# Merging the second chunk of an attention sum over one block of nodes, two rows at a time

## The chip, the cores and the metric

The kernel runs on one core of one Trainium2 chip. The metric is the device time of one execution in microseconds, lower is better. Five engines work in parallel, each through its own queue of instructions in program order: TensorE (PE, matmuls), VectorE (DVE), ScalarE (ACT), GpSimd (POOL) and SyncE (SP, transfers). PE writes only to PSUM, a small accumulation memory; everything else lives in SBUF.

## The reference

The input is x, 64 graphs of 256 nodes with 128 features, and one 256 x 256 adjacency matrix. Four layers follow, each after a layer norm and a relu, each added onto x. The change concerns layer 0 alone, a graph attention whose score of a pair of nodes needs all 256 hidden features:

```python
    s1 = jnp.einsum('bkf,ef->bke', x, W1)
    s2 = jnp.einsum('bkf,ef->bke', x, W2)
    pre = s1[:, :, None, :] + s2[:, None, :, :] + b_lin
    h = jnp.where(pre >= 0, pre, ALPHA * pre)
    e = jnp.einsum('bije,e->bij', h, a) + bias
    attn = jax.nn.softmax(e, axis=2)
    out = jax.nn.sigmoid(jnp.einsum('bij,bjf->bif', attn, x))
```

For every graph that is a tensor of 256 x 256 x 256 (receiver i, sender j, feature e) that goes through a leaky relu and is summed over e with the weights a. Layer 1 is a gated aggregation with elu, layer 2 a tanh-capped attention, layer 3 five steps of a gated recurrence; they take the rest of the time.

## The kernel before

**Layer 0's algebra.** The leaky relu is split into a linear part, which is one matmul with v2_rep, and 0.8 times a relu, up to terms that the softmax ignores. The absolute value of a[e] is folded into the weights, so that only the sign of a[e] is left for the sum over features. The features are permuted (place, perm): those with a positive a come first, and neighbours in this order fall into the same partition of two chunks, chunk 0 holding the even places and chunk 1 the odd ones. Sign by sign the two chunks then agree in every partition, except in one if the number of positive signs is odd: the odd column. In the kernel before, this column is zeroed in chunk 1 (a_abs1) and its share is brought back for both blocks of nodes by the row term left and the matrix left2: in senders, two instructions at L570 per graph add min(left_ps, bound) to the adjacency and give adj_l, which softmax0 adds to the scores at L755.

**A tile.** For a receiver node i and a chunk, a tile of 128 features x 256 senders holds max(s2, -s1[i]). The 256 receivers are two blocks (ic = 0, 1) of 128 nodes, and a block is four groups (g) of 32 nodes. A row t takes the nodes 32 g + t of both blocks: eight tiles per chunk, held in one buffer r of 128 x 4 x 2 x 256 (there are 11). ACT makes a tile with a relu (L687), POOL with tensor_scalar (L692), and DVE makes all eight, or four, in one instruction (L669).

**A batch.** One filled buffer is a batch. PE sums it over the features with four matmuls of 512 columns (L740), one for each group g. The stationary operand is a window of 32 columns of a_win, which holds plus or minus 0.8 in its column t and zeros elsewhere, so that the result falls into row t of the group's 32 rows of e_ps. A graph's scores accumulate in e_ps over all its batches.

**Merging.** A row needs one batch for each chunk, or a single batch if chunk 1 is added onto chunk 0's tile before PE reads it. Pairs.begin merges a row if at least SPARE = 5 finished batches wait for PE. DVE then adds chunk 1's tile onto chunk 0's tile in one instruction (Pairs.merge, L709), eight times for a row; that instruction makes chunk 1's tile as it adds it.

**The order of the work.** The order is written by a planner when the program is built (manual_schedule). It keeps a clock for each engine (class Model, with costs such as TILE, WHOLE, HALF, MERGE and BATCH in ns), and always emits the step that can start first: a step of one of the chains (generators that hold the small steps of the layers: ahead for the next graph's head and senders, behind for softmax0, others for layers 1 to 3), a batch for PE, a merge for DVE, or a new tile for a free ACT, POOL or DVE. All graphs' layer-0 work is thus spread over the whole execution, and the other layers' steps lie between its batches on each engine. The helper mm (L109) issues every other matmul as four of 32 output columns.

Of the kernel before, what the change touches and what calls it, by code (L numbers as in the profile page):

```python
# [27 lines left out]
def flat(t):  # L28
    return t.rearrange("p a b -> p (a b)")
# [26 lines left out]
def kernel(ctx: ExitStack, tc: tile.TileContext, ins: dict, out: bass.AP):  # L56
# [32 lines left out]
    def dve(n, pointers=0, more=0):  # L89
        model.op("dve", 66 + n * 1.042 + 60 * pointers + more)  # L90
        return nc.vector
# [128 lines left out]
    def constants0():  # L220
# [7 lines left out]
        def col(name):  # L228
            return constant([P, 2], name)
# [21 lines left out]
        dve(2).tensor_tensor(dif, bef[:, 0:2], neg_pl, ALU.subtract)  # L251
        dve(2).tensor_tensor(dif, dif, sgn, ALU.mult)
        dve(2).tensor_tensor(place, dif, neg_pl, ALU.add)

        last, a_abs1 = col("last"), col("a_abs1")
        dve(2).tensor_scalar(last, place, n_pos, None, ALU.is_equal)
        dve(2).tensor_tensor(a_abs1, a_abs, last, ALU.mult)
        dve(2).tensor_tensor(a_abs1, a_abs, a_abs1, ALU.subtract)
        perm = lent([P, 2, 2, P], "perm", "e_t", 2)
        for src in range(2):  # L260
            for c, size in ((0, a_abs), (1, a_abs1)):
                dve(P).tensor_scalar(
                    perm[:, src, c, :], places[:, c, :], place[:, src : src + 1],
                    size[:, src : src + 1], ALU.is_equal, ALU.mult,
                )
        yield "pe"
        b_ps = psum([P, 2], "blin_ps")
# [40 lines left out]
            dve(1).tensor_scalar(w, w, 1.6, -0.8, ALU.mult, ALU.add)  # L308


        odd = constant([P, 1], "odd")
        dve(1).tensor_scalar(odd, p_two[:, 1:2], n_pos, None, ALU.is_equal)
        yield "pe"
# [4 lines left out]
        dve(1).tensor_copy(odd_all, p)  # L318
        left, left_n, left_nb = col("left"), col("left_n"), col("left_nb")
        dve(2).tensor_tensor(left, a_col, last, ALU.mult)  # L320
        dve(2).tensor_scalar(left, left, odd_all, 0.8, ALU.mult, ALU.mult)
        dve(2).tensor_scalar(left_n, left, -1.0, None, ALU.mult)
        dve(2).tensor_tensor(left_nb, left_n, blin, ALU.mult)
        for c in range(2):
# [233 lines left out]
    def senders(b, of, to):  # L558

        h_t = flat(of["h_t"][:, 2 * b : 2 * b + 2, :])  # L560
        if "bound" not in of:
            yield from bounds(of)
        yield "pe", settled
        p = psum_h([P, N], "left_ps")
        mm(p, lhsT=left2, rhs=h_t, start=True, stop=True)
        for ic in range(2):
            yield "dve", None, of["bound_at"]
            if ic == 0:
                adj_l = ap.tile([P, 2, N], F32, tag="adj_l", name="adj_l", bufs=3)
            dve(N, 1).scalar_tensor_tensor(  # L570
                adj_l[:, ic, :], p, of["bound"][:, 2 * b + ic : 2 * b + ic + 1], adj_n[:, ic, :],
                ALU.min, ALU.add,
            )
        to["adj_l"] = adj_l
        if "s2" in to:
            return
        yield "pe"
        p = psum_h([P, 2, N], "s2_ps")
        for ec in range(2):
            mm(p[:, ec, :], lhsT=w_p[:, 1, bass.ts(ec, P)], rhs=h_t, start=True, stop=True)  # L580
        yield "act"
        s2 = ap.tile([P, 2, N], F32, tag="s2", name="s2")
        act(2 * N).copy(s2, p)
        to.update(s2=s2, s2_ps=p)

    class Pairs:

        def __init__(self, g, b, of, snd):
            self.g, self.b, self.of, self.snd = g, b, of, snd
            self.row = 0
            self.todo = []
            self.merges = []
            self.batches = []
            self.opened = False
            self.owned, self.by_act = {}, 0

            self.s1n_v = of["s1n"][:, :, bass.ts(b, N)].rearrange(  # L600
                "p c (k g t) -> p c g k t", k=2, g=4
            )

        def more(self):
            return self.todo or self.row < 32
# [4 lines left out]

        def begin(self):
            waiting = sum(x["halves"] == 2 for x in self.batches)
            merged = waiting >= SPARE
            for ec in range(1 if merged else 2):
                batch = {"t": self.row, "ec": ec, "merged": merged, "halves": 0, "ready": 0.0}
                self.todo += [(batch, ec, 0), (batch, ec, 1)]
            self.row += 1

        def finished(self):

# [21 lines left out]
            batch["halves"] += 1  # L642
            batch["ready"] = max(batch["ready"], model.t[who] + LAG[who])

        def nodes(self, t, g2):

            return [
                (g, ic, self.b * N + ic * P + 32 * g + t)
                for g in (2 * g2, 2 * g2 + 1) for ic in range(2)
            ]  # L650

        def make(self, who):

            if not self.todo:
                self.begin()
            batch, ec, g2 = self.todo.pop(0)
            if g2 == 0:
                batch["r"] = rp.tile([P, 4, 2, N], F32, tag="r", name="r")
                self.batches.append(batch)
            r, t = batch["r"], batch["t"]  # L660
            s2 = self.snd["s2"] if who == "pool" else self.own(who)
            s1, s1n = self.of["s1"], self.of["s1n"]
            if who == "dve":
                whole = g2 == 0 and self.todo and self.todo[0][0] is batch
                if whole:
                    self.todo.pop(0)
                n = 4 if whole else 2
                model.op("dve", model.WHOLE if whole else model.HALF)
                nc.vector.tensor_tensor(  # L669
                    r[:, 2 * g2 : 2 * g2 + n, :, :],  # L670
                    s2[:, ec : ec + 1, :].unsqueeze(1).to_broadcast([P, n, 2, N]),
                    self.s1n_v[:, ec, 2 * g2 : 2 * g2 + n, :, t : t + 1].to_broadcast([P, n, 2, N]),
                    ALU.max,
                )
                if whole:
                    if batch["merged"]:
                        self.merges.append((model.t[who] + LAG[who], batch, 0))
                        g2 = 1
                    else:
                        self.whole(batch, who)  # L680
            else:
                for g, ic, i in self.nodes(t, g2):
                    if g > 2 * g2 or ic:
                        yield
                    if who == "act":
                        model.op("act", model.TILE["act"] + 42 * (s2 is self.snd["s2"]))
                        nc.scalar.activation(  # L687
                            r[:, g, ic, :], s2[:, ec, :], AF.Relu, bias=s1[:, ec, i : i + 1]
                        )
                    else:  # L690
                        model.op("pool", model.TILE["pool"])
                        nc.gpsimd.tensor_scalar(  # L692
                            r[:, g, ic, :], s2[:, ec, :], FLT_MAX, s1n[:, ec, i : i + 1],
                            ALU.min, ALU.max,
                        )
            if batch["merged"]:
                self.merges.append((model.t[who] + LAG[who], batch, g2))
            else:
                self.whole(batch, who)

        def merge(self):

            _, batch, g2 = self.merges.pop(0)
            r, t = batch["r"], batch["t"]
            for g, ic, i in self.nodes(t, g2):
                if g > 2 * g2 or ic:
                    yield
                model.op("dve", model.MERGE)
                nc.vector.scalar_tensor_tensor(  # L709
                    r[:, g, ic, :], self.own("dve")[:, 1, :], self.of["s1n"][:, 1, i : i + 1],  # L710
                    r[:, g, ic, :], ALU.max, ALU.add,
                )
            self.whole(batch, "dve")
# [16 lines left out]
        def multiply(self):  # L730
            if not self.opened:
                self.open()
                self.opened = True
            batch = self.next_batch()
            self.batches.remove(batch)
            self.over = not self.batches and not self.more()
            t, r = batch["t"], batch["r"]
            model.op("pe", model.BATCH)
            for g in range(4):
                nc.tensor.matmul(  # L740
                    self.e_ps[bass.ts(g, 32), :, :].rearrange("p a b -> p (a b)"),
                    lhsT=a_win[:, batch["ec"], 31 - t : 63 - t], rhs=flat(r[:, g, :, :]),
                    start=False, stop=self.over, skip_group_check=True,
                )

    def softmax0(g, b, of, e_ps, snd):

# [2 lines left out]
        for ic in range(2):  # L750
            yield "dve", lambda: "adj_l" in snd

            if ic == 0:
                nmax = sp.tile([P, 2], F32, tag="nmax", name="nmax")
            dve(N, more=10).tensor_tensor_reduce(  # L755
                e_ps[:, ic, :], e_ps[:, ic, :], snd["adj_l"][:, ic, :], -1.0, FLT_MAX,
                ALU.add, ALU.min, nmax[:, ic : ic + 1],
            )
        for ic in range(2):
# [529 lines left out]
```

## Time and profile before

| | |
|---|---|
| median of three runs | 5038.96 us (5033.29, 5038.96, 5039.4) |
| the profiled execution | 5032.98 us |
| its span, first to last instruction | 5031.1 us |
| mean granted TensorE clock | 0.999 |
| instructions DVE / ACT / POOL | 9026 / 12984 / 10725 |
| matmul records (two for each program matmul) | 57307 |
| bytes moved | 28.02 MB, mean 6 GB/s |

A line of the page's groups gives line, engine and operation, written tile <- read tiles, shapes and count, then busy time in us and the mean ns of one, then the idle time of the engine just before such instructions and what ended most of it. Busy time counts a moment once even where instructions of one engine overlap. The timeline merges equal instructions that follow each other on an engine: start in us, the time from the first start to the last end, engine, line, names, shapes and count. A row of waits gives who waited for whom, us in total, how often, and the longest.

### The profile page before, as it was taken

To read this page: it belongs to the slowest core of one execution; us is meant where nothing else is said; L and a number is where in the kernel's file an instruction comes from. 1 tells how busy PE (TensorE), PEld (TensorE's weight loads), DVE (VectorE), ACT (ScalarE), POOL (GpSimd) and SP (SyncE) were. 2 spreads that over 40 slices of the span, in tenths; PEclk is the share of its full clock that TensorE was granted. 3 is DMA by queue.
4 is the path that set the end of the run, shared out by engine and by line. 5 is a ranking of instruction groups with operands and counts; after the bars stand their busy time and mean duration, and the time that the engine had idled before them with its cause. 6 is when DMAs were issued, how large, how long until landed. Compare 5 with 4: busy or idle time off the path is not lost. (4 is left out here: it accounts for less than half of the span.)

```text
span 5031.1 us, 151796 instructions
## 1 busy us (share of the span) xinstructions
PE 4975.7 (99%) x57307; PEld 1949.9 (39%) x57307; DVE 4926.9 (98%) x9026; ACT 4945.2 (98%) x12984; POOL 4817.0 (96%) x10725
## 2 busy tenths in 40 slices
PE   9999999999999999999999999999999999999998
PEld 3334433333334333343333333333333443333433
DVE  9999999999999999999999999999999999999995
ACT  8999999999999999999999999999999999999995
POOL 8999999999999999999999999999999999999991
PEclk9999999999999999999999999999999999999999
DMA  0000000000000000000000000000000000000000
GB/s 23 4 5 2 5 6 6 6 2 6 6 6 6 2 6 6 6 6 2 6 6 6 6 2 6 6 6 6 4 6 6 6 4 3 5 4 4 4 4 8
DMA packets 56017, 28.02 MB, mean 6 GB/s; under 512 B 20336, under 2 KB 55280, under 8 KB 55280
## 3 DMA queue, kind: packets, MB, share of 16 engines
q1 hardware_dynamic: 54736, 18.04, 1.5%
q8 instruction: 449, 7.36, 0.6%
q14 instruction: 288, 2.36, 0.2%
q10 hardware_dynamic: 544, 0.26, 0.0%
HBM read 9.84 MB, written 8.45 MB: 4 GB/s over the span
## 5 line engine op out<-in xcount | busy, mean ns | idle before, releaser
L692 POOL TENSOR_SCALAR r<-s,s1n 128x256 f32<-128x256 f32 x10100 | 4567.7, 476 | 55.7 <-PE e_ps L740 28.0
L687 ACT ACTIVATE r<-s_act,s 128x256 f32<-128x256 f32 x9736 | 4360.0, 1073 | 4.6 <-PE e_ps L740 4.3
L740 PE MATMUL e_ps<-r,a_win 128*32 128x512 f32 x27824 | 3251.8, 593 | 8.8 <-DVE r L709 4.0
L669 DVE TENSOR_TENSOR r<-s_ps,s1n 128x2048 f32<-128x2048 f32 (+1 forms) x1210 | 2120.7, 1790 | 0.8 <-POOL r L692 0.8
L709 DVE SCALAR_TENSOR_TENSOR r<-s_ps,s1n,r 128x256 f32<-128x256 f32 x4944 | 2013.3, 471 | 0.2
L740 PEld LDWEIGHTS e_ps<-r,a_win 128*32 128x32 f32 x27824 | 918.8, 110 | 1721.4 <-issue 1290.3
L687 ACT ACTIVATE r<-s,s 128x256 f32<-128x256 f32 x512 | 318.8, 1234 | 0.0
L458 ACT ACTIVATE h<-x,bsh,brs 128x128 f32<-128x128 f32 x384 | 264.3, 1040 | 10.5 <-POOL bsh L452 5.0
L109 PE MATMUL m_ps<-adj_t,hn 128*32 128x256 f32 x4096 | 253.6, 381 | 1.1 <-ACT hn L1066 1.1
L1025 ACT ACTIVATE m_ps<-gate_ps,br 128x512 f32<-128x512 f32 (+1 forms) x170 | 194.7, 1145 | 14.2 <-PE gate_ps L109 13.1
L1045 ACT ACTIVATE hv_ps<-hv_ps,bh 128x512 f32<-128x512 f32 (+1 forms) x170 | 198.7, 1169 | 7.2 <-PE hv_ps L109 7.2
L1043 ACT ACTIVATE gate_ps<-gate_ps,bz 128x512 f32<-128x512 f32 (+1 forms) x170 | 203.8, 1200 | 1.1 <-PE gate_ps L109 1.1
L1015 ACT COPY m_t<-m_ps 128x512 f32<-128x512 f32 (+1 forms) x170 | 193.9, 1140 | 6.1 <-PE m_ps L109 5.6
L109 PEld LDWEIGHTS m_ps<-adj_t,hn 128*32 128x32 f32 x4096 | 140.0, 110 | 126.2 <-issue 46.1
L109 PE MATMUL gate_ps<-m_t,t_w_w 128*32 128x512 f32 (+1 forms) x1360 | 172.7, 572 | 2.6 <-ACT m_t L1015 2.2
L109 PE MATMUL gate_ps<-m_t,w_t 128*32 128x512 f32 (+1 forms) x1360 | 172.5, 568 | 2.5 <-ACT m_ps L1025 2.4
L109 PE MATMUL hv_ps<-rh,u_th 128*32 128x512 f32 (+1 forms) x1360 | 172.1, 567 | 2.1 <-DVE rh L1028 2.0
L109 PE MATMUL hv_ps<-m_t,t_w_w 128*32 128x512 f32 (+1 forms) x1360 | 172.4, 568 | 0.0
L1066 ACT COPY hn<-hn_ps 128x512 f32<-128x512 f32 (+1 forms) x136 | 153.2, 1127 | 8.7 <-PE hn_ps L116 8.6
L109 PE MATMUL gate_ps<-hf,u_t 128*32 128x512 f32 (+1 forms) x1088 | 141.9, 571 | 0.0
L109 PE MATMUL s_ps<-h0t,w_p 128*32 128x256 f32 (+1 forms) x1568 | 136.2, 446 | 1.2 <-ACT h0t L474 0.5
L450 POOL TENSOR_TENSOR brs<-bve,neg_half 128x4 f32<-128x4 f32 (+1 forms) x136 | 133.5, 982 | 0.0
(214 smaller groups left out, 4781.2 us busy)
## 6 DMA issues: line engine op xcount, KB each, us to landing
xt<-in_x_dram SPq DMA_DIRECT2D x30, 256.0 KB
out_dram<-y SPq DMA_DIRECT2D x30, 256.0 KB
row<-rows SPq DMA_DIRECT2D x128, 0.5 KB
xt<-in_x_dram SPq DMA_DIRECT2D x4, 128.0 KB
out_dram<-y SPq DMA_DIRECT2D x4, 128.0 KB
bound<-row SPq DMA_DIRECT2D x30, 2.0 KB
raw_L_gnn_w_w<-in_L_gnn_w_w_dram SPq DMA_DIRECT2D x3, 128.0 KB
adj_n<-in_adj_dram ACTq DMA_DIRECT2D x1, 256.0 KB
```

What stands on the lines that cost most here:

```text
L109: nc.tensor.matmul(out[bass.ts(c, 32), :], lhsT=lhsT[:, bass.ts(c, 32)], rhs=rhs, **flags)
L458: act(P, 2, 1).activation(h[:, g, :], xt[:, g, :], AF.Relu, bias=shift[:, g : g + 1], scale=rstd[:, g : g + 1],)
L669: nc.vector.tensor_tensor(r[:, 2 * g2 : 2 * g2 + n, :, :], s2[:, ec : ec + 1, :].unsqueeze(1).to_broadcast([P, n, 2, N]), self.s1n_v[:, ec ...
L687: nc.scalar.activation(r[:, g, ic, :], s2[:, ec, :], AF.Relu, bias=s1[:, ec, i : i + 1])
L692: nc.gpsimd.tensor_scalar(r[:, g, ic, :], s2[:, ec, :], FLT_MAX, s1n[:, ec, i : i + 1], ALU.min, ALU.max,)
L709: nc.vector.scalar_tensor_tensor(r[:, g, ic, :], self.own("dve")[:, 1, :], self.of["s1n"][:, 1, i : i + 1], r[:, g, ic, :], ALU.max, ALU.add,)
L740: nc.tensor.matmul(self.e_ps[bass.ts(g, 32), :, :].rearrange("p a b -> p (a b)"), lhsT=a_win[:, batch["ec"], 31 - t : 63 - t], rhs=flat(r[ ...
L1015: act(W).copy(m_t, m_ps)
L1025: act(W, 1).activation(t_r, g_ps, AF.Tanh, bias=br, scale=0.5)
L1043: act(W, 1).activation(t_z, g_ps, AF.Tanh, bias=bz, scale=0.5)
L1045: act(W, 1).activation(cand, hv_ps, AF.Tanh, bias=bh)
L1066: act(W).copy(hn, tp)
```

## The change

Chunk 1 is added onto chunk 0 only for the first block of nodes (ic = 0), and two rows, t and t+1, are merged together. Such a pair makes three batches: row t and row t+1 of chunk 0, each with four merged tiles in block 0 and four plain ones in block 1, and one batch "two" with chunk 1's tiles of block 1 for both rows. Chunk 1 keeps its odd column (a_abs1 goes). In block 0, chunk 1 is always summed with chunk 0's signs, merged or not, and in block 1 with its own. So only block 0 has a wrong sign in the odd column, and the mending is done for it alone: one instruction at the former L570 with a factor of 1.6 in place of 0.8, and softmax0 adds plain adj_n to block 1. As the two blocks of a chunk-1 batch need different windows of a_win, such a batch is eight matmuls of 256 columns in place of four of 512; a chunk-0 batch stays four of 512. The planner's costs are unchanged. Empty lines are left out of the diff.

```diff
@@ -251,17 +251,14 @@
         dve(2).tensor_tensor(dif, bef[:, 0:2], neg_pl, ALU.subtract)
         dve(2).tensor_tensor(dif, dif, sgn, ALU.mult)
         dve(2).tensor_tensor(place, dif, neg_pl, ALU.add)
-        last, a_abs1 = col("last"), col("a_abs1")
+        last = col("last")
         dve(2).tensor_scalar(last, place, n_pos, None, ALU.is_equal)
-        dve(2).tensor_tensor(a_abs1, a_abs, last, ALU.mult)
-        dve(2).tensor_tensor(a_abs1, a_abs, a_abs1, ALU.subtract)
         perm = lent([P, 2, 2, P], "perm", "e_t", 2)
         for src in range(2):
-            for c, size in ((0, a_abs), (1, a_abs1)):
+            for c in range(2):
                 dve(P).tensor_scalar(
                     perm[:, src, c, :], places[:, c, :], place[:, src : src + 1],
-                    size[:, src : src + 1], ALU.is_equal, ALU.mult,
+                    a_abs[:, src : src + 1], ALU.is_equal, ALU.mult,
                 )
         yield "pe"
         b_ps = psum([P, 2], "blin_ps")
@@ -318,7 +316,7 @@
         dve(1).tensor_copy(odd_all, p)
         left, left_n, left_nb = col("left"), col("left_n"), col("left_nb")
         dve(2).tensor_tensor(left, a_col, last, ALU.mult)
-        dve(2).tensor_scalar(left, left, odd_all, 0.8, ALU.mult, ALU.mult)
+        dve(2).tensor_scalar(left, left, odd_all, 1.6, ALU.mult, ALU.mult)
         dve(2).tensor_scalar(left_n, left, -1.0, None, ALU.mult)
         dve(2).tensor_tensor(left_nb, left_n, blin, ALU.mult)
         for c in range(2):
@@ -563,14 +561,11 @@
         yield "pe", settled
         p = psum_h([P, N], "left_ps")
         mm(p, lhsT=left2, rhs=h_t, start=True, stop=True)
-        for ic in range(2):
-            yield "dve", None, of["bound_at"]
-            if ic == 0:
-                adj_l = ap.tile([P, 2, N], F32, tag="adj_l", name="adj_l", bufs=3)
-            dve(N, 1).scalar_tensor_tensor(
-                adj_l[:, ic, :], p, of["bound"][:, 2 * b + ic : 2 * b + ic + 1], adj_n[:, ic, :],
-                ALU.min, ALU.add,
-            )
+        yield "dve", None, of["bound_at"]
+        adj_l = ap.tile([P, N], F32, tag="adj_l", name="adj_l", bufs=3)
+        dve(N, 1).scalar_tensor_tensor(
+            adj_l, p, of["bound"][:, 2 * b : 2 * b + 1], adj_n[:, 0, :], ALU.min, ALU.add
+        )
         to["adj_l"] = adj_l
         if "s2" in to:
             return
@@ -600,6 +596,9 @@
             self.s1n_v = of["s1n"][:, :, bass.ts(b, N)].rearrange(
                 "p c (k g t) -> p c g k t", k=2, g=4
             )
+            self.s1n_b = of["s1n"][:, :, bass.ts(b, N)].rearrange(
+                "p c (k g t) -> p c k g t", k=2, g=4
+            )
         def more(self):
             return self.todo or self.row < 32
@@ -610,11 +609,19 @@
         def begin(self):
             waiting = sum(x["halves"] == 2 for x in self.batches)
-            merged = waiting >= SPARE
-            for ec in range(1 if merged else 2):
-                batch = {"t": self.row, "ec": ec, "merged": merged, "halves": 0, "ready": 0.0}
+            merged = waiting >= SPARE and self.row < 31
+            t = self.row
+            if merged:
+                kinds = ((t, 0, True, False), (t + 1, 0, True, False), (t, 1, False, True))
+            else:
+                kinds = ((t, 0, False, False), (t, 1, False, False))
+            for t, ec, on_top, two in kinds:
+                batch = {
+                    "t": t, "ec": ec, "merged": on_top, "two": two, "halves": 0, "ready": 0.0
+                }
                 self.todo += [(batch, ec, 0), (batch, ec, 1)]
-            self.row += 1
+            self.row += 2 if merged else 1
         def finished(self):
@@ -642,11 +649,12 @@
             batch["halves"] += 1
             batch["ready"] = max(batch["ready"], model.t[who] + LAG[who])
-        def nodes(self, t, g2):
+        def nodes(self, batch, g2):
+            t, two = batch["t"], batch["two"]
             return [
-                (g, ic, self.b * N + ic * P + 32 * g + t)
-                for g in (2 * g2, 2 * g2 + 1) for ic in range(2)
+                (g, k, self.b * N + 32 * g + t + (P + k if two else k * P))
+                for g in (2 * g2, 2 * g2 + 1) for k in range(2)
             ]
         def make(self, who):
@@ -665,11 +673,15 @@
                 if whole:
                     self.todo.pop(0)
                 n = 4 if whole else 2
+                if batch["two"]:
+                    s1n = self.s1n_b[:, ec, 1, 2 * g2 : 2 * g2 + n, t : t + 2].unsqueeze(3)
+                else:
+                    s1n = self.s1n_v[:, ec, 2 * g2 : 2 * g2 + n, :, t : t + 1]
                 model.op("dve", model.WHOLE if whole else model.HALF)
                 nc.vector.tensor_tensor(
                     r[:, 2 * g2 : 2 * g2 + n, :, :],
                     s2[:, ec : ec + 1, :].unsqueeze(1).to_broadcast([P, n, 2, N]),
-                    self.s1n_v[:, ec, 2 * g2 : 2 * g2 + n, :, t : t + 1].to_broadcast([P, n, 2, N]),
+                    s1n.to_broadcast([P, n, 2, N]),
                     ALU.max,
                 )
                 if whole:
@@ -679,7 +691,7 @@
                     else:
                         self.whole(batch, who)
             else:
-                for g, ic, i in self.nodes(t, g2):
+                for g, ic, i in self.nodes(batch, g2):
                     if g > 2 * g2 or ic:
                         yield
                     if who == "act":
@@ -701,9 +713,11 @@
         def merge(self):
             _, batch, g2 = self.merges.pop(0)
-            r, t = batch["r"], batch["t"]
-            for g, ic, i in self.nodes(t, g2):
-                if g > 2 * g2 or ic:
+            r = batch["r"]
+            for g, ic, i in self.nodes(batch, g2):
+                if ic:
+                    continue
+                if g > 2 * g2:
                     yield
                 model.op("dve", model.MERGE)
                 nc.vector.scalar_tensor_tensor(
@@ -736,12 +750,22 @@
             self.over = not self.batches and not self.more()
             t, r = batch["t"], batch["r"]
             model.op("pe", model.BATCH)
-            for g in range(4):
-                nc.tensor.matmul(
-                    self.e_ps[bass.ts(g, 32), :, :].rearrange("p a b -> p (a b)"),
-                    lhsT=a_win[:, batch["ec"], 31 - t : 63 - t], rhs=flat(r[:, g, :, :]),
-                    start=False, stop=self.over, skip_group_check=True,
-                )
+            if batch["two"]:
+                parts = ((1, t, 1, 0), (1, t + 1, 1, 1))
+            elif batch["ec"]:
+                parts = ((0, t, 0, 0), (1, t, 1, 1))
+            else:
+                parts = ((slice(0, 2), t, 0, slice(0, 2)),)
+            for ic, t, sign, k in parts:
+                for g in range(4):
+                    to, of = self.e_ps[bass.ts(g, 32), ic, :], r[:, g, k, :]
+                    if len(parts) == 1:
+                        to, of = to.rearrange("p a b -> p (a b)"), flat(of)
+                    nc.tensor.matmul(
+                        to, lhsT=a_win[:, sign, 31 - t : 63 - t], rhs=of,
+                        start=False, stop=self.over, skip_group_check=True,
+                    )
     def softmax0(g, b, of, e_ps, snd):
@@ -753,7 +777,7 @@
             if ic == 0:
                 nmax = sp.tile([P, 2], F32, tag="nmax", name="nmax")
             dve(N, more=10).tensor_tensor_reduce(
-                e_ps[:, ic, :], e_ps[:, ic, :], snd["adj_l"][:, ic, :], -1.0, FLT_MAX,
+                e_ps[:, ic, :], e_ps[:, ic, :], adj_n[:, 1, :] if ic else snd["adj_l"], -1.0, FLT_MAX,
                 ALU.add, ALU.min, nmax[:, ic : ic + 1],
             )
         for ic in range(2):
```

## The prediction

> **What bounds the kernel now.** I read the page first: engine shares, then the costliest groups.
>
> ```profile
> span 5031.1 us, 151796 instructions
> PE 4975.7 (99%) x57307; PEld 1949.9 (39%) x57307; DVE 4926.9 (98%) x9026; ACT 4945.2 (98%) x12984; POOL 4817.0 (96%) x10725
> ...
> L692 POOL TENSOR_SCALAR r<-s,s1n 128x256 f32<-128x256 f32 x10100 | 4567.7, 476 | 55.7 <-PE e_ps L740 28.0
> L687 ACT ACTIVATE r<-s_act,s 128x256 f32<-128x256 f32 x9736 | 4360.0, 1073 | 4.6 <-PE e_ps L740 4.3
> L740 PE MATMUL e_ps<-r,a_win 128*32 128x512 f32 x27824 | 3251.8, 593 | 8.8 <-DVE r L709 4.0
> L709 DVE SCALAR_TENSOR_TENSOR r<-s_ps,s1n,r 128x256 f32<-128x256 f32 x4944 | 2013.3, 471 | 0.2
> ```
>
> No engine stands out: all four are busy for 96 to 99% of the span, because the planner hands row tiles to whichever engine is free. POOL and ACT make tiles (L692, L687), DVE makes tiles (L669) and merges (L709), and PE eats them (L740). What a change is worth is therefore a balance: what it adds to each engine against the idle time that engine really has. The busy shares cannot give that, since records overlap: a mean of 593 ns is a matmul's latency, not its place in the stream. So next the timeline, where the distance between starts is the true cost.
>
> ```profile
> 4705.39 1.93 PE L740 MATMUL e_ps<-r,a_win 128*32 128x512 f32 x16
> 4707.13 1.91 PE L109 MATMUL m_ps<-adj_t,hn 128*32 128x256 f32 x32
> 4708.86 1.04 PE L109 MATMUL gate_ps<-hf,u_t 128*32 128x512 f32 x8
> 4709.72 1.90 PE L740 MATMUL e_ps<-r,a_win 128*32 128x512 f32 x16
> 4711.43 1.04 PE L109 MATMUL gate_ps<-m_t,t_w_w 128*32 128x512 f32 x8
> ```
>
> Every program matmul leaves two records, and four of them, one per 32-column strip, run side by side. Sixteen records of 512 columns take 4711.43 - 4709.72 = 1.71 us, so four take 0.43 us and one batch of L740 (four matmuls, eight records) 0.86 us. Thirty-two records of 256 columns take 4708.86 - 4707.13 = 1.73 us: 0.216 us for four. The medians over the whole trace are 429 and 216 ns.
>
> With these pitches PE's true work follows: 35,024 records of 512 columns at 429/4 ns, 12,256 of 256 at 216/4, 8,496 of 128 or 129 at about 109/4, and 1,419 transposes at 109 ns with some 0.11 us lost on entering a group and 0.15 us in and behind it, are 4902 us. Of the span of 5031 that leaves 129 us in which PE had nothing to do: 23 us before 434 us (start-up), 79 us between 434 and 4594, 1 us between 4594 and 4850, 26 us in the tail. So PE, at "99%", has 1.9% of idle in the long middle, too short each time to show, and almost none (0.4%) in the stretch 4594 to 4850.
>
> The other engines' pitches come from the same view.
>
> ```profile
> 2124.90 4.00 DVE L709 SCALAR_TENSOR_TENSOR r<-s_ps,s1n,r 128x256 f32<-128x256 f32 x10
> 2128.82 0.16 DVE L968 RECIPROCAL rv<-o_ps 128x2 f32<-128x2 f32 x1
> ...
> 2129.93 2.28 DVE L669 TENSOR_TENSOR r<-s_ps,s1n 128x2048 f32<-128x2048 f32 x1
> 2132.12 0.47 DVE L439 BATCH_NORM_STATS2 bst<-x 128x6 f32<-128x128 f32 x2
> ...
> 2017.86 21.69 POOL L692 TENSOR_SCALAR r<-s,s1n 128x256 f32<-128x256 f32 x48
> 2039.52 1.28 POOL L863 TENSOR_TENSOR x1b<-x,bm_bc 128x512 f32<-128x512 f32 x1
> ...
> 2023.24 6.26 ACT L687 ACTIVATE r<-s_act,s 128x256 f32<-128x256 f32 x14
> 2028.23 1.54 ACT L855 COPY y<-y_ps 128x256 f32<-128x256 f32 x1
> ```
>
> A merge costs 3.92/10 = 0.392 us of DVE, a whole production on DVE (eight tiles) 2.19 to 2.20, half of one 1.13 (trace median), a tile on POOL 21.66/48 = 0.451 and one on ACT 4.99/14 = 0.356. Last, the waits of DVE:
>
> ```profile
> DVE adj_l L570 <- PE left_ps L109: 7.0, 14, 1.2
> DVE e_ps L755 <- PE e_ps L740: 6.5, 12, 1.4
> ```
>
> In the middle stretch (434 to 4594 us) DVE waits only some 27 us, half of it for PE in these two rows. DVE and ACT are the full engines there; PE is the one with a little room.
>
> **The change, part by part.**
>
> *Mending (senders, softmax0).* One of two adj_l additions a graph goes: 64 DVE instructions. The instruction has a merge's form and its distance to the next one has the same median, 0.392 us: -25.1 us of DVE. softmax0 reads adj_n for the second block instead: same shape, no change. Two 128x2 instructions of the setup go: nothing.
>
> *Merges (begin, nodes, merge).* Before, a merged row costs 8 merges and spares 8 tiles and one batch. After, a pair of merged rows costs 2 x 4 merges, makes 24 tiles instead of 32 and feeds three batches instead of four: again 8 merges for 8 tiles and one batch. The exchange rate is the same; what differs is how often the planner takes it. The built programs say: merges 4944 to 4472 (618 packets of eight to 559), POOL tiles 10,100 to 9,992, ACT tiles on s_act 9736 to 9644, DVE whole productions 659 to 748, halves 551 to 541. That is POOL -108 x 0.451 = -48.7 us, ACT -92 x 0.356 = -32.8 us, DVE -472 x 0.392 + 89 x 2.198 - 10 x 1.131 = -0.7 us, with the mending -25.8 us.
>
> *Batches (multiply).* L740's matmuls go from 13,912 of 512 columns (3478 batches) to 8192 of 512 (2048 batches of chunk 0) and 11,912 of 256 (1489 batches of chunk 1): 59 batches more, 59 x 0.858 = +50.6 us of PE. Each chunk-1 batch is now eight matmuls of half the width: 4 x 216 = 864 ns against 2 x 429 = 858, +6 ns x 1489 = +8.9 us. Together +59.5 us of PE.
>
> One rival price for this width: do the weight loads, twice as many per column, still hide? The 256-column rows above load 32 columns for every matmul and run at half the 512-column pitch, so I take yes. The Trainium skill, page "TensorE: Matmul & The Clock Gate", Part 3 (The mechanism), speaks against the change: loads overlap running matmuls only where the row group differs, and here all loads use all 128 rows. By its load formula (columns over 1.2, so an estimate of 27 ns for 32) two more exposed load rounds a batch would be 53 ns x 1489, about 79 us more; the trace's 216 against 429 disagrees.
>
> *Code.* The queue that brings instructions moved 449 packets (7.36 MB) with 0.6% of 16 engines' span, 1.07 us each; PE's program grows by 21%, some 95 packets. They come ahead of use, so nothing; were each one waited for, 100 us.
>
> *Waits.* PE runs in order: an e_ps batch that waits for its tiles holds the chain matmuls behind it (m_ps, gate_ps, left_ps), and through them DVE and ACT. A later PE also frees r buffers later; POOL's waits for that are 28 us now, and POOL and ACT gain 49 and 33 us to take more.
>
> *The sum.* Three engines get lighter by 26 to 49 us, PE gets heavier by 59.5 us. DVE alone would allow -26 us. PE decides: 4902 + 59.5 = 4961.5 us of work, plus its idle time. Start-up keeps about 20 of its 23 us, the tail 27, the late stretch 1. For the middle, bounds: at the fill of the best stretch seen, 0.4%, 17 us; unchanged, 79 us. With DVE relieved and more finished batches queued before PE I take a value near the fullest row, 0.5%, 21 us. Then the span is 4961.5 + 20 + 21 + 1 + 27 = 5030.5 us against 5031.1: no change. The profiled execution took 5032.98 us, 1.9 more than its span; the median of the three runs is 6 us above it. I set 5034, between the two. The gain on DVE is bought with PE's last idle time. (No change means within 0.2%, 10 us, about what a measurement of this kernel can tell.)
>
> **Rivals.**
>
> *Faster: PE runs without gaps.* If PE, now the last engine, always has a finished batch, the middle idle falls towards 5 us and the start-up's excess goes too: 4961.5 + 18 + 5 + 27 = 5011.5, execution some 5013. For it: 200 us windows of the middle with 0.4 to 0.8 us of idle exist already. Against: most windows have 2 to 7 us, and three engines are then full together.
>
> *Slower: the idle time cannot be filled.* Merging now comes in packets of two rows, whose two on-top batches both need DVE before PE may start, so PE may still run out of ready batches, and its chain matmuls still wait for ACT and DVE. Each us of idle left beyond 31 in the middle (0.75%) puts the time over +10 us; at 45 us left it is 5054 for the span, 5056 for the execution; with all 79, 5090. For it: idle in the middle is spread over many small waits today, left_ps and the transposes among them. Against: the planner merges less, which means that more batches go straight to PE.
>
> *Slower, and not what it says: half-width matmuls cost more than half.* Four strips here stream four different operands, where m_ps streams the same one. The row left_ps, also 256 wide, has a quarter of its groups at 240 ns. At 240 it would be 1489 x 4 x 24 ns = 143 us, some 5170.
>
> **How the numbers follow.** No change 0.38, its own range 5023 to 5043; PE without gaps 0.28; idle that stays 0.29; dear half-width matmuls 0.05. Faster 0.28, same 0.38, slower 0.34. The range has to reach into both neighbours: 5010 leaves out a tenth below at most, and 5068 takes in idle of about 57 us and leaves out the rest and the dear matmuls.
>
> **What would show it.** In the profile after: 256-column groups of e_ps at 216 ns per four (each step of +24 ns is 143 us); 8192 and 11,912 matmuls; PE's work 4961 us and its idle in the middle near 20 us; POOL's share down by about a point, with more waiting for PE at e_ps. PE with more than 40 us idle there, or DVE waits for PE well above 27 us, would prove the balance wrong.

## The result, and the profile after

The changed kernel takes 5024.06 us (median of 11 runs, 5022.82 to 5029.97) against 5038.88 us before (11 runs, 5033.29 to 5041.98): ratio 0.9973, 95% interval 0.9965 to 0.9982, faster by 0.27%. The profiled execution took 5022.82 us with a span of 5021.0 us. Of the 14.8 us between the medians, 10.1 are found between the two spans; the profiled execution of before is one of its fastest, 6 us under the median, that of after only 1.2 under its own. So the two traces show two thirds of the gain.

The page of the changed kernel, engine shares and the groups that answer to those shown before:

```profile
span 5021.0 us, 176445 instructions
PE 4988.7 (99%) x69691; PEld 2295.2 (46%) x69691; DVE 4902.5 (98%) x8567; ACT 4916.4 (98%) x12892; POOL 4769.3 (95%) x10617
...
L704 POOL TENSOR_SCALAR r<-s,s1n 128x256 f32<-128x256 f32 x9992 | 4519.8, 476 | 103.1 <-PE e_ps L765 55.4
L699 ACT ACTIVATE r<-s_act,s 128x256 f32<-128x256 f32 x9644 | 4188.5, 894 | 12.5 <-PE e_ps L765 12.3
L765 PE MATMUL e_ps<-r,a_win 128*32 128x256 f32 (+1 forms) x40208 | 3259.8, 467 | 3.4 <-DVE r L681 3.3
...
L723 DVE SCALAR_TENSOR_TENSOR r<-s_ps,s1n,r 128x256 f32<-128x256 f32 x4472 | 1838.2, 471 | 1.0 <-POOL r L704 0.7
```

DVE is busy 24.4 us less (4926.9 to 4902.5). PE's busy time rises by 13 us only, because "busy" covered its small gaps already. The waits have changed sides: tile makers that wait for PE to free a buffer went from 28.0 to 55.4 us on POOL and from 4.3 to 12.3 us on ACT.

The timeline of PE, where starts give the pitch:

```profile
2006.88 1.91 PE L765 MATMUL e_ps<-r,a_win 128*32 128x256 f32 x24
2008.60 1.04 PE L109 MATMUL gate_ps<-m_t,t_w_w 128*32 128x512 f32 x8
```

The 24 records are a half-width batch (16 of 256 columns) and a full one (8 of 512; equal names are merged under the first shape). They take 1.72 us, which is 4 x 0.216 + 2 x 0.429. Over the whole trace the median of four half-width records of a batch is 216 ns, so in this trace the weight loads (110 ns each) hide with four different operands too. With these pitches PE's work is 4961.9 us and its idle time 59 us, against 4902 and 129 before. In the middle stretch (434 to 4594 us) 79 us of idle have become 12. The largest waits of PE there that its busy time shows were at the mending's own matmul; the row of the kernel before, in this stretch:

```profile
L109 PE MATMUL left_ps<-h0t,left 128*32 128x256 f32 x432 | 35.1, 387 | 10.3 <-DVE r L709 6.1 <-DVE r L669 4.1
```

In the changed kernel these 10.3 us are 1.2. Each engine's busy time in that stretch, of the kernel before and then of the changed one (columns: length, PE, PEld, DVE, ACT, POOL, clock, DMA share, GB/s):

```profile
434.00:4594.00 4160.00, 4136.30 (x47406) 1620.17 (x47402) 4128.38 (x7660) 4154.06 (x10893) 4084.18 (x9073) 1.00 0.02 5
```
```profile
434.00:4594.00 4160.00, 4158.77 (x57888) 1904.08 (x57881) 4129.93 (x7312) 4146.03 (x10862) 4064.78 (x9030) 1.00 0.02 5
```

DVE keeps its 30 us of gaps while doing less per graph; ACT, with 6 us of gaps before, has 14 after; POOL's grow from 76 to 95. PE alone closes up. (These gaps are those that the busy time shows; where records overlap, as ACT's do, they are a lower bound.)

### The profile page after: what moved, and what is told of

It is laid out like the page before. It is cut to its first block, busy times and chain, and to the rows that moved or that the text cites. A ratio compares the mean times of both kernels' runs of the same rounds, so it can differ in the third digit from the quotient of the medians.

```text
span 5021.0 us, 176445 instructions
## 1 busy us (share of the span) xinstructions
PE 4988.7 (99%) x69691; PEld 2295.2 (46%) x69691; DVE 4902.5 (98%) x8567; ACT 4916.4 (98%) x12892; POOL 4769.3 (95%) x10617
## 4 chain that ended last, share of the span: by engine, by line
PE 95%; DVE 3%; ACT 1%; issue 1%; POOL 0%; DMA 0%; DVEq 0%; POOLq 0%; ACTq 0%
PE e_ps L765 59%; PE gate_ps L109 8%; PE hv_ps L109 6%; PE m_ps L109 5%; PE s_ps L109 3%; PE o_ps L109 2%; PE e_ps L109 2%; DVE r L681 2%; PE rc_ps L109 2%; PE hn_ps L116 1%; PE rsum_ps L109 1%; PE e_ps L116 1%; PE h_t_ps L116 1%; PE left_ps L109 1%; PE th_ps L109 1%; PE g_ps L109 1%
## 5 line engine op out<-in xcount | busy, mean ns | idle before, releaser
L704 POOL TENSOR_SCALAR r<-s,s1n 128x256 f32<-128x256 f32 x9992 | 4519.8, 476 | 103.1 <-PE e_ps L765 55.4
L699 ACT ACTIVATE r<-s_act,s 128x256 f32<-128x256 f32 x9644 | 4188.5, 894 | 12.5 <-PE e_ps L765 12.3
L765 PE MATMUL e_ps<-r,a_win 128*32 128x256 f32 (+1 forms) x40208 | 3259.8, 467 | 3.4 <-DVE r L681 3.3
L681 DVE TENSOR_TENSOR r<-s_ps,s1n 128x2048 f32<-128x2048 f32 (+1 forms) x1289 | 2311.0, 1828 | 3.4 <-PE e_ps L765 3.3
L765 PEld LDWEIGHTS e_ps<-r,a_win 128*32 128x32 f32 x40208 | 1286.3, 110 | 1579.1 <-issue 863.8
L723 DVE SCALAR_TENSOR_TENSOR r<-s_ps,s1n,r 128x256 f32<-128x256 f32 x4472 | 1838.2, 471 | 1.0 <-POOL r L704 0.7
L699 ACT ACTIVATE r<-s,s 128x256 f32<-128x256 f32 x512 | 304.3, 1073 | 0.0
L456 ACT ACTIVATE h<-x,bsh,brs 128x128 f32<-128x128 f32 x384 | 230.8, 867 | 8.6 <-POOL bsh L450 7.9
L1049 ACT ACTIVATE m_ps<-gate_ps,br 128x512 f32<-128x512 f32 (+1 forms) x170 | 166.4, 981 | 12.8 <-PE gate_ps L109 8.3
L1067 ACT ACTIVATE gate_ps<-gate_ps,bz 128x512 f32<-128x512 f32 (+1 forms) x170 | 174.3, 1026 | 2.9 <-PE gate_ps L109 2.9
L1039 ACT COPY m_t<-m_ps 128x512 f32<-128x512 f32 (+1 forms) x170 | 164.4, 967 | 5.2 <-PE m_ps L109 5.2
L1090 ACT COPY hn<-hn_ps 128x512 f32<-128x512 f32 (+1 forms) x136 | 130.6, 960 | 17.7 <-PE hn_ps L116 17.5
```

The lines of the kernel that those rows point to most:

```text
L456: act(P, 2, 1).activation(h[:, g, :], xt[:, g, :], AF.Relu, bias=shift[:, g : g + 1], scale=rstd[:, g : g + 1],)
L681: nc.vector.tensor_tensor(r[:, 2 * g2 : 2 * g2 + n, :, :], s2[:, ec : ec + 1, :].unsqueeze(1).to_broadcast([P, n, 2, N]), s1n.to_broadcast ...
L699: nc.scalar.activation(r[:, g, ic, :], s2[:, ec, :], AF.Relu, bias=s1[:, ec, i : i + 1])
L704: nc.gpsimd.tensor_scalar(r[:, g, ic, :], s2[:, ec, :], FLT_MAX, s1n[:, ec, i : i + 1], ALU.min, ALU.max,)
L723: nc.vector.scalar_tensor_tensor(r[:, g, ic, :], self.own("dve")[:, 1, :], self.of["s1n"][:, 1, i : i + 1], r[:, g, ic, :], ALU.max, ALU.add,)
L765: nc.tensor.matmul(to, lhsT=a_win[:, sign, 31 - t : 63 - t], rhs=of, start=False, stop=self.over, skip_group_check=True,)
```

## Experiments

Theory A: the gain needs the tile makers (DVE above all) to get lighter, and PE's idle time pays for it. Theory B: the gain is only that PE is filled by merging less; the mending does not matter. Ratios are to the kernel before, as executed beside each experiment; the changed kernel stands at 0.9973 (0.9965 to 0.9982). A ratio carries about 0.0009 either way, so two kernels that lie less than some 6 us apart are not told apart by their times.

### e1: merging less, nothing else

```diff
-SPARE = 5
+SPARE = 6
```

> The kernel before with SPARE = 6: it merges less often, and nothing else is changed. Its program has 38 batches more, 304 merges fewer, 52 ACT tiles and 68 POOL tiles fewer: PE +33 us, POOL -31 us, ACT -19 us, DVE -304 x 0.392 + 40 x 2.198 + 26 x 1.131 = -2 us. Theory A (the changed kernel gains because DVE got lighter while PE's idle time paid for it): DVE stays full here, so -2 us, ratio 0.9995, although PE is filled up. Theory B (the gain is the filling of PE alone, by merging less, and the mending does not matter): about half of the changed kernel's gain for half of its additional batches, some -7 us, ratio 0.9985.

Ratio 0.9997 (0.9988 to 1.0006): nothing, as A said. PE's work rose to 4935 us and its idle in the middle fell from 79 to 46, yet the time stayed. The page fits this: DVE's busy time is nearly the old one.

```profile
PE 4980.7 (99%) x57611; PEld 1902.4 (38%) x57611; DVE 4925.1 (98%) x8788; ACT 4929.3 (98%) x12932; POOL 4787.1 (95%) x10657
```

Filling PE by itself is worth nothing here; the 16 and 30 us that ACT and POOL lost became their idle time.

### e2: merging less, and one mending instruction

```diff
-SPARE = 5
+SPARE = 6
...
-        for ic in range(2):
-            yield "dve", None, of["bound_at"]
...
+        yield "dve", None, of["bound_at"]
+        adj_l = ap.tile([P, N], F32, tag="adj_l", name="adj_l", bufs=3)
+        dve(N, 1).scalar_tensor_tensor(
+            adj_l, p, of["bound"][:, 2 * b : 2 * b + 1], adj_n[:, 0, :], ALU.min, ALU.add
+        )
...
```

> The kernel before with SPARE = 6 and without the second mending instruction of a graph (block 1 gets plain adjacency: the odd column's share is left out there). No two-row merging, no half-width matmuls. Against before: DVE -15 us, ACT -23 us, POOL -27 us, PE +22 us. Theory A: DVE decides, -15 us, ratio 0.997, the same gain as the changed kernel without its split. Theory B: as e1 without the mending, -5 us, ratio 0.999.

Ratio 0.9984 (0.9975 to 0.9993), -8 us: between the two theories (-15 and -5). DVE's busy time fell by 15.5 us (to 4911.4), as predicted, but only half of that reached the end.

### e3: the mending put back into the changed kernel

```diff
...
+        yield "dve", None, of["bound_at"]
+        dve(N, 1).scalar_tensor_tensor(
+            adj_l[:, 1, :], p, of["bound"][:, 2 * b + 1 : 2 * b + 2], adj_n[:, 1, :], ALU.min, ALU.add
...
```

> The changed kernel with its second mending instruction put back (into a half of adj_l that nothing reads): 64 DVE instructions of 0.392 us more, with which the planner merges 80 times less. Against the changed kernel: PE +10 batches, +8.7 us, DVE +5 us. Theory A, with PE as the engine that ends last in the changed kernel: +9 us, ratio to before 0.999. Theory B (mending does not matter): 0.997 as the changed kernel.

Ratio 0.9981 (0.9972 to 0.9990): about 4 us worse than the changed kernel, where A said 9 and B nothing; the intervals overlap. PE's work is 4970 us, as expected. With the mending back the kernel is still faster than before, since the planner merges 552 times less than before and DVE is busy 4909.4 us, 17.5 less. By the ratios the mending instructions as such are the smaller part of the gain, some 4 of 14 us.

### e4: the changed kernel, merging more

```diff
-SPARE = 5
+SPARE = 4
```

> The changed kernel with SPARE = 4: it merges more, 27 batches fewer than the changed kernel. Against before: PE +36 us, DVE -20 us, ACT -23 us, POOL -29 us. If PE is the last engine of the changed kernel, it gets 23 us of room here and the time goes to DVE's bound: 5031 - 20 = 5011 us of span, ratio 0.996, faster than both kernels. If instead PE's late batches do not set the end, DVE's 6 us more and the additional merges show: +4 us against the changed kernel, ratio 0.998.

Ratio 0.9979 (0.9970 to 0.9987), some 3 to 4 us behind the changed kernel, with overlapping intervals: the second reading fits, and the hope for a faster version (0.996) fell. PE got its idle back (38 us in the middle), DVE is busy 4909.3 us, 6.8 more.

### e5 and e6: every batch in half-width matmuls

The same edit for both kernels, the order of all instructions unchanged; in the changed kernel:

```diff
-                parts = ((slice(0, 2), t, 0, slice(0, 2)),)
+                parts = ((0, t, 0, 0), (1, t, 0, 1))
```

> The kernel before with every batch as eight matmuls of 256 columns in place of four of 512; order and all else unchanged. PE gets 3478 x 6 ns = 21 us more work. Theory A (PE has 79 us of real idle time in the middle of the kernel before, in spite of 99% busy): it is swallowed, 0 to +4 us, ratio 1.000 to 1.001. Rival (PE at 99% busy is the bound already): +21 us, 1.004.

> The changed kernel with its chunk-0 batches also as eight matmuls of 256 columns; order and all else unchanged. PE gets 2048 x 6 ns = 12 us more. Theory A (PE's idle time is used up in the changed kernel, 12 us left in the middle): +10 us against the changed kernel, ratio to before 0.999. Rival (DVE is the bound and PE still has cover): 0 to +3 us, 0.997 to 0.998.

Before: 1.0004 (0.9995 to 1.0013), medians +3.3 us for 20.9 us of additional work (4902.2 to 4923.1). Changed kernel: 0.9987 (0.9978 to 0.9996) for 12.3 us (4961.9 to 4974.2): +10.1 us over its median, +9.8 by the spans, +7 by the ratios. The same 6 ns a batch are mostly swallowed in one kernel and mostly count in the other, though both pages say PE 99%. The times alone hardly tell the two effects apart (2 and 7 us by the ratios), but they agree with the idle time that the starts show in the middle, 79 us before and 12 after: PE had real idle time before and has used it up after.

### e7: merging more in the last three graphs

```diff
...
-            merged = waiting >= SPARE and self.row < 31
+            merged = waiting >= (SPARE if self.n < 61 else 3) and self.row < 31
```

> The changed kernel with SPARE = 3 for its last three graphs alone: there it merges three packets more, PE -2.6 us, in the stretch where PE is full and the other three idle. If PE sets the end from graph 62 on: -3 us against the changed kernel, ratio to before 0.9967, beyond both kernels by little. If the tail's chains set it: 0.

Ratio 0.9968 (0.9956 to 0.9980), the median that of the changed kernel (5024.05 us), the span 0.6 us shorter. It beats the kernel before, but not measurably the changed one: inconclusive, and the nearest thing to a better version that was found.

### e8: PE relieved in the last three graphs

```diff
...
+            if batch["ec"] and self.n >= 61 and not self.over:
+                parts = parts[:1]
...
```

> The changed kernel without the block-1 half of the chunk-1 batches' matmuls in the last three graphs (these sums are left out; nothing else changes, the order on DVE, ACT and POOL is the same): 212 matmuls of 256 columns, 53 groups of four, 53 x 0.432 = 23 us of PE less there. Theory A' (of the 28.7 us that the changed kernel leads at the start of graph 62, 18 are given back since PE alone is full over the last three graphs): -18 us against the changed kernel, ratio to before 0.9937. Rival (the lead is lost in the chains of the last group, which wait for one another whatever PE does): 0 to -3 us, 0.997.

Ratio 0.9960 (0.9948 to 0.9973), 4 us by the medians, 3.3 by the spans, 7 by the ratios (no more than the noise), for 23 us of PE's work: A' falls. Graph 62 starts 28.7 us earlier in the changed kernel's trace than before (4640.5 against 4669.2 us), its last batch only 10.6 earlier (4926.4 against 4937.0). PE is full over these three graphs, but that alone is not why the rest is late. The same stretches, changed kernel first, then e8:

```profile
4640.00:4732.00 92.00, 91.74 (x1280) 41.85 (x1276) 90.36 (x181) 86.48 (x220) 81.62 (x182) 1.00 0.02 5
4732.00:4830.00 98.00, 97.52 (x1321) 44.59 (x1314) 89.71 (x197) 93.13 (x239) 85.81 (x192) 1.00 0.02 5
4830.00:4926.00 96.00, 96.00 (x1317) 42.76 (x1312) 86.29 (x185) 83.15 (x214) 73.68 (x166) 1.00 0.02 5
```
```profile
4640.00:4732.00 92.00, 88.14 (x1174) 37.71 (x1169) 90.87 (x180) 87.38 (x223) 83.01 (x184) 1.00 0.02 5
4732.00:4830.00 98.00, 93.03 (x1198) 39.07 (x1194) 91.05 (x202) 94.40 (x242) 87.24 (x194) 1.00 0.02 5
4830.00:4926.00 96.00, 90.05 (x1166) 37.43 (x1159) 88.14 (x193) 83.99 (x217) 73.89 (x166) 1.00 0.02 5
```

PE's busy time falls by 14 us, and the other three engines get only 3 to 4 us busier in these 286 us. What they wait for there in the changed kernel is scattered (DVE at layer 3's df for ACT 7.7 us, at rh 4.3; POOL for buffers 19.3). The lead was also partly work put off: at that moment the changed kernel has 344 us of PE's work left by the pitches, the kernel before 324. Which of these waits costs the 18 us stays open.

### e9 to e12: one engine relieved or loaded, the order kept

Theory C: several engines are full at once, so work added to one counts and work taken from one does not. e9 drops the second mending instruction of the kernel before, but leaves it in the planner's account:

```diff
-            dve(N, 1).scalar_tensor_tensor(
+            dve(N, 1)
+            if ic == 0:
+                nc.vector.scalar_tensor_tensor(
...
```

> The kernel before without the second mending instruction of each graph, but planned as if it were there: the order of all other instructions is the old one (block 1's share of the odd column is left out). 64 x 0.392 = 25 us of DVE less, nothing else. Theory C (before the change, DVE, ACT and POOL are full together, and relieving one of them without a new plan gains little): 0 to -6 us, ratio 0.999 to 1.000. Rival (DVE alone is the bound): -20 us or more, 0.996.

Ratio 0.9998 (0.9989 to 1.0007): nothing. DVE's waits in the middle stretch grew from 27 to about 50 us; these rows stood at 6.5, 4.7 and 2.8 us before:

```profile
DVE e_ps L757 <- PE e_ps L742: 12.3, 20, 1.8
DVE xh_t L819 <- ACT elu_m L816: 10.3, 15, 1.1
...
DVE self_t L895 <- PE rsum_ps L109: 5.7, 9, 1.7
```

The 25 us taken from DVE came back as DVE waiting for ACT and PE. ACT's busy time leaves 5 us of gaps in the middle stretch, and from one tile to the next its starts are 0.357 us apart; what exceeds that by over 0.05 us adds up to under 2 us. It is still not quite full: from a tile to a step of a chain the usual distance is the same 0.357 us, but in 204 of 1472 cases it is over 0.05 us longer, 62 us in all (63 in the kernel before), and the overlapping records cover this.

e10 puts the second mending instruction back into the changed kernel, unplanned (a plain nc.vector call behind the first one, no step of its own):

> The changed kernel with the second mending instruction put back (nothing reads its result) but not planned for: 25 us of DVE more, the order of all else unchanged, PE's work unchanged. Theory C (DVE is full in the changed kernel too, beside PE): +15 to +25 us against the changed kernel, ratio to before 1.000 to 1.002. Rival (PE alone is the bound there, and DVE has cover): 0 to +4 us, 0.998.

Ratio 0.9981 (0.9972 to 0.9990), +5 us by the medians, +4 by the ratios, for 25 us of DVE: nearer the rival. DVE's idle in the middle, 30 us in the changed kernel, fell to 16 us and took in 14 us of it; it was not as full as C had it.

e11 drops the block-1 half of one chunk-1 batch a graph from the changed kernel, and e12 the remaining mending instruction as well:

```diff
+            if batch["ec"] and t >= 16 and not self.light and not self.over:
+                self.light, parts = True, parts[:1]
...
-        dve(N, 1).scalar_tensor_tensor(
-            adj_l, p, of["bound"][:, 2 * b : 2 * b + 1], adj_n[:, 0, :], ALU.min, ALU.add
-        )
...
+        dve(N, 1)
...
```

> The changed kernel without the block-1 half of one chunk-1 batch in each graph (these sums are left out): 64 x 0.432 = 28 us of PE less, spread over the whole run, the order of all else unchanged. Theory C (DVE and PE are full together, so that work on either counts when it is added, but taking it from one does not help): 0 to -6 us against the changed kernel, ratio to before 0.996 to 0.997. Rival (PE alone is the bound): -22 us, 0.993.

> The changed kernel with two things left out together, the order of all else unchanged: the block-1 half of one chunk-1 batch in each graph, as in e11 (PE -28 us), and the mending instruction that is left in each graph (DVE -25 us; both blocks get plain adjacency). Theory C' (PE and DVE are full together, so each alone gives little and both together give most): -15 to -20 us against the changed kernel, ratio to before 0.993 to 0.994. Rival (all four engines are tied by the written order, ACT and POOL too): no more than the two single effects, -4 to -8 us, 0.9960 to 0.9965.

e11: 0.9966 (0.9953 to 0.9978), some 3.6 us by the medians for 28 us of PE. e12: 0.9966 (0.9952 to 0.9979), no more than e11 although DVE is 25 us lighter on top. Both give less than a fifth of what one full engine would. In e12's middle stretch PE has 10 us of visible gaps and DVE 48 (in the changed kernel 1 and 30), while ACT is busy as before:

```profile
434.00:4594.00 4160.00, 4149.99 (x57468) 1893.38 (x57464) 4112.00 (x7257) 4150.54 (x10862) 4084.68 (x9030) 1.00 0.02 5
```

So C held in e9 and e11 and fell in e10, C' fell in e12, and the rival of e12 fits: with the order kept, what is taken from PE or DVE mostly comes back as their waiting. Whether ACT's own list of instructions is what holds the time is not shown. No run relieved ACT or POOL with the order kept, and ACT's starts in e12 still come 67 us late before steps of chains, against 69 in the changed kernel.

## Why the prediction was right or wrong

**The work was right.** PE's work was put at 4961.5 us and measured 4961.9; 8192 and 11,912 matmuls ran at the pitches named; DVE lost 24.4 us of busy time for the 25.8 predicted. The dear half-width matmul fell with the 216 ns. The code's growth (547 packets of the instruction queue for 449) shows no price, since PE's idle time shrank all the same.

**The idle time was sized too large.** The step that failed is PE's remaining idle. For start-up, middle, late stretch and tail I took 20 + 21 + 1 + 27 = 69 us; measured were 22.5 + 11.7 + 2.3 + 22.6 = 59 us. The middle closed to 0.28%, below the 0.4% of the best stretch seen, which I had taken as the lower bound and then exceeded for safety. These 10 us are the whole distance between the predicted span (5030.5) and the measured one (5021.0). The measured span lies halfway between "no change", the forecast, and the rival "PE runs without gaps" (5011.5), which came half true: the middle closed to 11.7 us where it had 5, the start-up kept 22.5 where it had 18, and only the tail was 4 us shorter than its 27. The time lies in the stated range, but "no change", meant as within 10 us, was missed: the medians differ by 14.8 us, beyond the interval. Placing the time 3.5 us above the span was right (measured 3.1). The other 5 us lie in the kernel before, whose median is 7.8 us above the span of its trace; the traces do not show why.

**The rival on the other side failed by its condition.** It needed over 31 us of idle left in the middle; merging two rows at a time left 12. e1 and e4, with 46 and 38 us left, show that such a state exists; e1 gained nothing, and e4 gained, by its ratio, somewhat less than the changed kernel.

**What the sum did not say.** "PE decides" treated PE as the only limit after the change and the lighter tile makers as mere room. It does not hold alone: e4 and e11 gave PE 23 and 28 us back, and the one did not gain and the other gained 4. The prediction also called ACT full; by its starts it had some 60 us left in the middle (e9). The runs speak for both sides being needed. Changes against the kernel before, each with a new plan (PE's work by counts and pitches, the time by the ratio, of 5039 us):

| kernel | DVE busy, us | PE's work, us | time, us |
|---|---|---|---|
| e1, merging less | -1.8 | +33 | -1.5 |
| e2, merging less and one mending | -15.5 | +22 | -8 |
| e3, changed kernel, mending twice | -17.5 | +68 | -10 |
| e4, changed kernel, merging more | -17.6 | +36 | -11 |
| the change | -24.4 | +60 | -14 |

In these five the time goes with DVE's relief, at a little over half of it, and not with PE's work. By tiles and pitches ACT lost 19 to 33 us and POOL 27 to 49, so DVE is the least relieved maker in each. That is a pattern in five kernels, whose times differ by little more than the noise, and not a proof. Less merging without less mending gains nothing (e1), both together do (e2). Less mending gains nothing in the old order (e9); with a new plan of its own it was not run. Nor was the kernel before with one mending and a SPARE over 6, so that the runs do not show whether the two-row merging is needed for the rest of the gain, or only the planner's merging less. (e3, with two rows but without the mending's saving, has two thirds of the gain, the intervals allowing less or more.) A part of DVE's relief is lost in the last three graphs, which give back 18 of 29 us; the cause is open.

## What to carry to other kernels

When several engines share one pool of work, price a change as a vector, one figure for each engine, and make a new plan with it: here relief counted when all the makers got lighter together, and the engine with real gaps paid for it. Measure that room from start-to-start distances, not from the busy share; a small equal load added to the suspected engine, as in e5 and e6, tests whether its gaps are real. Taking work from one engine in a fixed order told little here (e9, e11, e12): it came back as waiting.

## What was not expected of the hardware

The mean recorded duration of one and the same ACT tile instruction was 1073 ns before, 894 after and 881 to 1174 ns over the experiments, while its starts stayed 0.356 to 0.357 us apart (medians). It is the longest where ACT had the fewest gaps (e9, 1174 ns) and the shortest in e6 (881 ns), so ACT's busy share and mean ns say little on its load. What ACT still has to give was only to be seen in the starts.

In the middle of the kernel before, the granted TensorE clock fell to 0.5 for two stretches of 3.4 us, at 3129 and 3286 us, about where PE had waited 2.1 and 3.8 us at left_ps. Four records of 512 columns took 0.85 us there in place of 0.43. So some 3.4 of the 79 us of idle were a slow clock. The traces of e1, e2, e5 and e9, without the two-row merging, have such stretches in the middle too; the changed kernel's trace and those of the eight other experiments, all with it, have none.
